# Causal attention on one core: PSUM banks given out by a model of their readers, and maxima, exponentials and masks taken two or four heads at a time

## The chip, the cores and the metric

The kernel runs on one core of a Trainium2 chip. The metric is the device time of one launch in microseconds (us). The engines that matter are TensorE (PE, which multiplies matrices into the eight banks of PSUM; PEld is its loading of weights), VectorE (DVE) and ScalarE (ACT), which read PSUM, GpSimd (POOL), which here works on SBUF, and SyncE (SP), which issues DMAs. Each engine has its own instruction stream; an instruction that waits holds up all that stand behind it in that stream.

## The reference

One layer of a transformer on x of 2048 tokens by 256 features, in float32:

```python
q = x @ Wq;  c_kv = x @ Wkv_down;  k = c_kv @ Wk_up;  v = c_kv @ Wv_up    # 16 heads of 16
q, k: the last 12 of the 16 numbers of a head are rotated by their position
scores = (q . k) / 4, with -inf where the key is after the query
out = softmax(scores) . v
x = layernorm(x + out)
x = layernorm(x + experts(x) + shared(x))     # 16 experts, each token to its best two
```

## The kernel before, in words

**Tiling.** The 2048 tokens are four chunks (`c`) of 512. The 16 heads are four groups (`g`) of four heads. A head has 16 numbers and is padded to 32 partitions, so that the four heads of a group fill the 128 partitions. A product of one head uses 32 of TensorE's 128 rows, so that the products of the four heads of a group can run side by side in four row groups. Float32 products are done in passes; the trace has two records for one product.

**Two kinds of work.** Softmax needs the largest score of each query before the exponentials. `Maxima(g, c, t, kc)` is for one block `t` of 128 queries and one chunk `kc` of keys: four products of queries by keys (one for each head, tile `m`, 128 queries on partitions by `n` keys), and the maximum of each on DVE into `pm` (line L490). On the diagonal (`kc == c`) only `n = 128 (t + 1)` keys count, and one DVE operation adds a mask to all `n` columns and takes the maximum (L485; a short read of the accumulator follows each). `shift` turns the maxima and adds them to the queries (tile `qa`, L508), so that the later product has them already subtracted. `Weighted(g, c, kb, ...)` is for one block `kb` of 128 keys and one chunk of 512 queries: four products (tile `s`, 128 keys by 512 queries, fewer on the diagonal, where they begin at column `n0`), the exponential of each on ACT into an SBUF tile `p` of the pool `wkp` (L535), and on the diagonal a select on POOL which clears the upper triangle of a 128x128 block of `p` (L539).

**Values one step late.** `values` multiplies the four `p` by the values: four products into one bank (tile `av`). ACT copies `av` to `avs` the first time (L559), later to `more` (L566), which POOL adds to `avs` (L567); in steps with no Maxima DVE adds straight from PSUM (L563).

**The order.** The attention is a list, written out by hand, of 180 `steps`: each has a Maxima, a Weighted, or both. TensorE's instructions are kept in program order (`pe`, L139 to L143; every product has line L140 in the profile). A step with both goes

```python
for some, others in (((0, 1), (2, 3)), ((2, 3), (0, 1))):
    s.products(some)
    m.products(others)
    s.exponentials()
    m.reductions()
```

and then come `prior.values(...)`, the values of the step before, and what the table `at` puts behind this step: the loading and projection of later chunks and groups (`prologue`, `project_k`, `project_q`, `project_v`), `shift`, `finish`, and the routing of the experts.

**The banks.** `bank()` (L397) takes a tile of one bank, [128, 512] float32, from a pool of eight (`ps_sc`, L293), round robin. A step with both kinds takes eight for its products, and `av` takes a ninth. The pool `wkp` (L292) has nine tiles of 512 columns.

The experts follow after the attention, from about 593 us on; the change does not touch them.

Of the kernel before, what the change touches and what calls it, by code (L numbers as in the profile page):

```python
# [10 lines left out]
F32 = mybir.dt.float32  # L11
I32 = mybir.dt.int32
AF = mybir.ActivationFunctionType
ALU = mybir.AluOpType
AX = mybir.AxisListType
PSUM = bass.MemoryType.PSUM

P = 128
S, E = 2048, 256
H, HD, LAT = 16, 16, 64  # L20
NOPE, RD = 4, 12
G = 4
PAD = 32
LOW = HD + NOPE
# [17 lines left out]
SCALE = 0.25  # L42
EPS = 1e-5
NEG = -1.0e30


@with_exitstack
def block_kernel(
# [237 lines left out]
    with ExitStack() as att:  # L286
# [2 lines left out]
        wk1 = att.enter_context(tc.tile_pool(name="wk1", bufs=1))  # L289
        wk2 = att.enter_context(tc.tile_pool(name="wk2", bufs=2))  # L290
        wk3 = att.enter_context(tc.tile_pool(name="wk3", bufs=3))
        wkp = att.enter_context(tc.tile_pool(name="wkp", bufs=9))  # L292
        ps_sc = att.enter_context(tc.tile_pool(name="ps_sc", bufs=8, space=PSUM))  # L293

        wqs = [ap1.tile([P, 2, P], F32, tag=f"wqs{g}", name=f"wqs{g}") for g in range(G)]

# [97 lines left out]

        qs, ks, vs, qa, pm, avs = {}, {}, {}, {}, {}, {}

        def bank(name):  # L397
            return ps_sc.tile([P, CH], F32, tag="sc", name=name)

        def prologue(c):  # L400

            copy = nc.scalar.copy if c else nc.vector.tensor_copy
            for k in range(2):
                pt = bank(f"pt{c}_{k}")
                for t in range(4):
                    transpose(pt[:, t * P : (t + 1) * P], xr[c][:, t, k * P : (k + 1) * P], ident)
                copy(xT[c][:, k, :], pt)
            pc = bank(f"pc{c}")
            for k in range(2):
                matmul(  # L410
                    pc, lhsT=wkds[:, k, :], rhs=xT[c][:, k, :], start=(k == 0), stop=(k == 1)
                )
            copy(ckv[c], pc)
# [25 lines left out]

        def project_v(g, c):  # L440

            pv = [bank(f"pv{g}_{c}_{a}") for a in range(2)]
            for b in range(4):
                a = b % 2
                r = slice(a * LAT, (a + 1) * LAT)
                matmul(
                    pv[a][:, (b // 2) * P : (b // 2 + 1) * P],
                    lhsT=ckv[c][r, b * P : (b + 1) * P],
                    rhs=wvs[r, g * P : (g + 1) * P], start=True, stop=True,
                )  # L450
            v = kv.tile([P, CH], F32, tag="v", bufs=6, name=f"v{g}_{c}")
            for a in range(2):
                nc.scalar.copy(
                    v.rearrange("p (b a m) -> p b a m", a=2, m=P)[:, :, a, :],
                    pv[a][:, : 2 * P].rearrange("p (b m) -> p b m", m=P),
                )
            nc.gpsimd.memset(v.rearrange("p (h d) -> p h d", d=PAD)[:, :, ONE : ONE + 1], 1.0)
            vs[g, c] = v

        class Maxima:  # L460


            def __init__(self, g, c, t, kc):
                self.g, self.c, self.t, self.kc = g, c, t, kc
                self.n = CH if kc < c else (t + 1) * P
                if (g, c) not in pm:
                    pm[g, c] = wk3.tile([P, 4, 4, NCH], F32, tag="pm", name=f"pm{g}_{c}")

            def products(self, heads):
                g, c, t, kc, n = self.g, self.c, self.t, self.kc, self.n  # L470
                self.ps = {}
                for j in heads:
                    r = PAD * j
                    self.ps[j] = bank(f"m{g}_{c}_{t}_{kc}_{j}")
                    matmul(
                        self.ps[j][:, :n], lhsT=qs[g, c][r : r + PAD, t * P : (t + 1) * P],
                        rhs=ks[g, kc][r : r + PAD, :n], start=True, stop=True,
                    )

            def reductions(self):  # L480
                t, kc, n = self.t, self.kc, self.n
                for j, ps in self.ps.items():
                    to = pm[self.g, self.c][:, t, j, kc : kc + 1]
                    if kc == self.c:
                        nc.vector.tensor_tensor_reduce(  # L485
                            out=ps[:, :n], in0=ps[:, :n], in1=qmask[:, CH - n :], scale=1.0,
                            scalar=3.0 * NEG, op0=ALU.add, op1=ALU.max, accum_out=to,
                        )
                    else:
                        nc.vector.tensor_reduce(to, ps, AX.X, ALU.max)  # L490

        def negated(g, c):
            nm = wk1.tile([P, 4, 4, PAD], F32, tag="nm", name=f"nm{g}_{c}")
# [16 lines left out]
        class Weighted:  # L510
# [3 lines left out]
            def __init__(self, g, c, kb, first, last):  # L514
                self.g, self.c, self.kb, self.first, self.last = g, c, kb, first, last
                self.n0 = max(0, kb - 4 * c) * P
                self.pr = {}

            def products(self, heads):
                g, c, kb, n0 = self.g, self.c, self.kb, self.n0  # L520
                self.ps = {}
                for j in heads:
                    r = PAD * j
                    self.ps[j] = bank(f"s{g}_{c}_{kb}_{j}")
                    matmul(
                        self.ps[j][:, n0:],
                        lhsT=ks[g, kb // 4][r : r + PAD, (kb % 4) * P : (kb % 4 + 1) * P],
                        rhs=qa[g, c][r : r + PAD, n0:], start=True, stop=True,
                    )

            def exponentials(self):
                g, c, kb, n0 = self.g, self.c, self.kb, self.n0
                for j, ps in self.ps.items():
                    pr = wkp.tile([P, CH], F32, tag="pr", name=f"p{g}_{c}_{kb}_{j}")
                    nc.scalar.activation(pr[:, n0:], ps[:, n0:], AF.Exp, scale=SCALE)  # L535
                    if kb >= 4 * c:

                        diag = pr[:, n0 : n0 + P]
                        nc.gpsimd.affine_select(  # L539
                            out=diag, in_=diag, pattern=[[1, P]], base=0, channel_multiplier=-1,  # L540
                            compare_op=ALU.is_ge, fill=0.0,
                        )
                    self.pr[j] = pr

            def values(self, alone):


                g, c, kb, n0 = self.g, self.c, self.kb, self.n0
                pv = bank(f"av{g}_{c}_{kb}")
                for j in range(4):  # L550
                    r = PAD * j
                    o = (kb % 4) * P + r
                    matmul(
                        pv[r : r + PAD, n0:], lhsT=vs[g, kb // 4][:, o : o + PAD],
                        rhs=self.pr[j][:, n0:], start=True, stop=True,
                    )
                if self.first:
                    avs[g, c] = wk2.tile([P, CH], F32, tag="avs", name=f"avs{g}_{c}")
                    nc.scalar.copy(avs[g, c], pv)  # L559
                    return  # L560
                to = avs[g, c][:, n0:]
                if alone:
                    nc.vector.tensor_tensor(to, to, pv[:, n0:], ALU.add)  # L563
                else:
                    more = wk2.tile([P, CH], F32, tag="more", name=f"more{g}_{c}_{kb}")
                    nc.scalar.copy(more[:, n0:], pv[:, n0:])  # L566
                    nc.gpsimd.tensor_tensor(to, to, more[:, n0:], ALU.add)  # L567

        def finish(g, c):
            po = ps_sc.tile([P, 4, 4, PAD], F32, tag="sc", name=f"po{g}_{c}")  # L570
            for t in range(4):
                transpose(
                    po[:, t].rearrange("p h d -> p (h d)"), avs[g, c][:, t * P : (t + 1) * P], ident
                )
            rs = wk2.tile([P, 4, 4, 1], F32, tag="rs", name=f"rs{g}_{c}")
            nc.vector.reciprocal(rs, po[:, :, :, ONE : ONE + 1])
            oh = wk2.tile([P, 4, 4, HD], F32, tag="oh", name=f"oh{g}_{c}")
            nc.vector.tensor_tensor(oh, po[:, :, :, :HD], rs.to_broadcast([P, 4, 4, HD]), ALU.mult)
            xg = xr[c][:, :, g * 4 * HD : (g + 1) * 4 * HD]
            adder = nc.vector if g == G - 1 else nc.gpsimd  # L580
            adder.tensor_tensor(xg, xg, oh.rearrange("p t h d -> p t (h d)"), ALU.add)
            if g == G - 1:
                for t in range(4):
                    st = wk2.tile([P, 6], F32, tag="st", name=f"st{c}_{t}")
                    nc.vector.bn_stats(st, xr[c][:, t, :E])
                    nc.vector.bn_aggr(mv[:, 4 * c + t, :], st)
# [129 lines left out]
        while step < len(steps) or prior or at:  # L716
            m, s = steps[step] if step < len(steps) else (None, None)
            m = m and Maxima(*m)
            s = s and Weighted(*s, step == s_first[s[:2]], step == s_last[s[:2]])
            if m and s:  # L720
                for some, others in (((0, 1), (2, 3)), ((2, 3), (0, 1))):

                    s.products(some)
# [371 lines left out]
```

## Time and profile before

| | |
|---|---|
| time, median of 3 runs | 808.76 us (806.41 to 810.42) |
| profiled execution: time | 803.1 us |
| profiled execution: span, mean granted TensorE clock | 801.1 us, 0.993 |
| instructions | 14999 |
| exponentials (L535), ACT | 640, 292.6 us busy, 540 ns mean |
| maxima off the diagonal (L490), DVE | 384, 237.5 us, 681 ns |
| masked maxima (L485), DVE | 256, 118.3 us, 521 ns |
| selects (L539), POOL | 256, 70.5 us, 297 ns |

All durations come from the one profiled execution. Its span is the time from the first to the last instruction; the time of the same execution is 2.0 us longer, and the median of the runs is 5.7 us above that time. "Busy" is the sum over an engine's instructions; neighbours on one engine can overlap in the records, since one instruction begins before the result of the one ahead of it is wholly written. A row of the form `out<-in` names the tiles that an instruction writes and reads; an arrow `<-` after an idle time names what the engine waited for.

### The profile page before, as it was taken

Reading aid. Unit: us, or ns where it says so; the run is one execution under the profiler, and the core shown is the slowest. Engines: PE = TensorE matmul, PEld = TensorE weight load, DVE = VectorE, ACT = ScalarE, POOL = GpSimd, SP = SyncE. Lnnn points to the kernel's source line nnn. Section 1 sums busy time; section 2 is a strip of 40 time slices with the busy share of each in tenths; the row PEclk is TensorE's granted clock in tenths of the full one; section 3 lists DMA queues with packets and bytes.
Section 4 is the critical chain, followed back from the end, with each engine's and each line's share of the span. In section 5 each row is a group of like instructions: output and inputs, shape, how many; then the busy total and the mean of one; then the engine's idle time right before and its main releaser. Section 6 shows DMA issues by size and latency. Waiting matters only on the chain. (4 is left out here: it accounts for less than half of the span.)

```text
span 801.1 us, 14999 instructions
## 1 busy us (share of the span) xinstructions
PE 771.5 (96%) x5086; PEld 361.3 (45%) x5086; DVE 547.1 (68%) x1489; ACT 445.0 (56%) x997; POOL 323.0 (40%) x557
## 2 busy tenths in 40 slices
PE   7999999999999999999999999999989899999985
PEld 3443433444333344543334453444336466666543
DVE  2768888887687887777788678788775433333276
ACT  1143646377775786766688668875742033333345
POOL 2032524434355454635455454461661333333300
PEclk9999999999999999999999999999999999999998
DMA  5469999991000000001000000000225322222172
GB/s 147 130 174 327 310 301 304 294 301 54 2 1 1 1 2 1 2 19 37 1 2 2 1 2 2 1 2 2 80 84 141 107 80 86 82 86 70 37 230 85
DMA packets 67378, 71.88 MB, mean 90 GB/s; under 512 B 4736, under 2 KB 61539, under 8 KB 67302
## 3 DMA queue, kind: packets, MB, share of 16 engines
q1 hardware_dynamic: 62286, 61.77, 27.7%
q0 software_dynamic: 3552, 8.43, 3.0%
q10 hardware_dynamic: 1464, 0.72, 0.4%
q8 instruction: 41, 0.67, 0.4%
q14 instruction: 35, 0.29, 0.1%
HBM read 26.44 MB, written 45.78 MB: 90 GB/s over the span
## 5 line engine op out<-in xcount | busy, mean ns | idle before, releaser
L535 ACT ACTIVATE p<-s 128x512 f32<-128x512 f32 (+3 forms) x640 | 292.6, 540 | 128.2 <-PE m L140 79.0
L140 PE MATMUL m<-k,q 32*128 32x512 f32 (+3 forms) x1280 | 303.9, 566 | 0.8 <-DVE rot L423 0.5
L140 PE MATMUL s<-qa,k 32*128 32x512 f32 (+3 forms) x1280 | 279.4, 556 | 1.8 <-DVE avs L563 0.7
L490 DVE TENSOR_REDUCE pm<-m 128x1 f32<-128x512 f32 x384 | 237.5, 681 | 44.4 <-PE m L140 44.0
L567 POOL TENSOR_TENSOR avs<-avs,more 128x512 f32<-128x512 f32 (+3 forms) x125 | 136.7, 1094 | 167.3 <-ACT more L566 163.8
L140 PEld LDWEIGHTS s<-qa,k 32*128 32x128 f32 x1280 | 107.1, 184 | 117.6 <-ACT p L535 67.6
L140 PE MATMUL av<-p,v 128*32 128x512 f32 (+3 forms) x1280 | 154.2, 540 | 1.9 <-DVE base L244 1.2
L140 PEld LDWEIGHTS m<-k,q 32*128 32x128 f32 x1280 | 122.7, 184 | 44.5 <-issue 11.9
L485 DVE CUSTOM_DVE_ANT_0 m<-m,qmask 128x512 f32<-128x512 f32 (+3 forms) x256 | 118.3, 521 | 29.1 <-PE m L140 26.1
L566 ACT COPY more<-av 128x512 f32<-128x512 f32 (+3 forms) x125 | 65.6, 525 | 38.3 <-PE av L140 30.4
L539 POOL TENSOR_SCALAR_AFFINE_SELECT p<-p 128x128 f32<-128x128 f32 x256 | 70.5, 297 | 38.2 <-ACT p L535 36.4
L931 POOL DMA_INDIRECT yg<-yb,to x42 | 41.4, 985 | 88.2 <-ACT yb L923 44.1
L140 PEld LDWEIGHTS av<-p,v 128*32 128x32 f32 x1280 | 27.1, 108 | 104.1 <-ACT p L535 54.2
L140 PE MATMUL ph<-w,xbT 128*128 x168 | 60.3, 482 | 2.4 <-DVE xbT L884 1.7
L903 DVE TENSOR_TENSOR rh<-ru,ph 128x176 f32<-128x176 f32 x42 | 14.2, 338 | 53.7 <-ACT ru L901 53.7
L140 PE MATMUL h<-xT,cs 128*128 128x512 f32 (+1 forms) x96 | 43.6, 599 | 4.9 <-DVE sh L794 2.0
L901 ACT ACTIVATE ru<-ph 128x176 f32<-128x176 f32 x42 | 13.3, 318 | 59.3 <-PE ph L140 59.3
L140 PE MATMUL py<-w2r,hT 88*128 x168 | 43.4, 380 | 0.7 <-ACT hT L910 0.7
L278 POOL DMA_INDIRECT xg<-xr,slot x32 | 31.1, 971 | 31.1 <-issue 19.8
L140 PEld LDWEIGHTS ph<-w,xbT 128*128 128x128 f32 x168 | 28.5, 189 | 20.8 <-issue 11.6
L428 POOL TENSOR_TENSOR k<-rot 128x512 f32<-128x512 f32 x16 | 20.3, 1267 | 42.5 <-DVE rot L426 42.5
L140 PEld LDWEIGHTS py<-w2r,hT 88*128 88x128 f32 x168 | 31.7, 189 | 12.0 <-ACT hT L910 1.2
(147 smaller groups left out, 633.3 us busy)
## 6 DMA issues: line engine op xcount, KB each, us to landing
xg<-hot SPq DMA_DIRECT2D x16, 2064.0 KB
w<-in_w_dram SPq DMA_DIRECT2D x4, 1408.0 KB
xb<-xg SPq DMA_DIRECT2D x42, 129.0 KB
got<-yg SPq DMA_DIRECT2D x8, 512.0 KB
w2r<-in_w_dram SPq DMA_DIRECT2D x2, 1408.0 KB
xr<-in_x_dram SPq DMA_DIRECT2D x4, 512.0 KB
out_dram<-o SPq DMA_DIRECT2D x8, 256.0 KB
cs<-in_rope_dram SPq DMA_DIRECT2D x16, 80.0 KB
```

Source lines behind the costliest of these rows:

```text
L140: tc.keep_in_program_order(op(*args, **kw))
L278: put = nc.gpsimd.indirect_dma_start(out=xg[:, :], out_offset=bass.IndirectOffsetOnAxis(ap=slot[:, j, i : i + 1], axis=0), in_=xr[c][:, t, ...
L428: nc.gpsimd.tensor_tensor(ks[g, c], tmp[:, 0, :], tmp[:, 1, :], ALU.add)
L485: nc.vector.tensor_tensor_reduce(out=ps[:, :n], in0=ps[:, :n], in1=qmask[:, CH - n :], scale=1.0, scalar=3.0 * NEG, op0=ALU.add, op1=ALU.m ...
L490: nc.vector.tensor_reduce(to, ps, AX.X, ALU.max)
L535: nc.scalar.activation(pr[:, n0:], ps[:, n0:], AF.Exp, scale=SCALE)
L539: nc.gpsimd.affine_select(out=diag, in_=diag, pattern=[[1, P]], base=0, channel_multiplier=-1, compare_op=ALU.is_ge, fill=0.0,)
L566: nc.scalar.copy(more[:, n0:], pv[:, n0:])
L567: nc.gpsimd.tensor_tensor(to, to, more[:, n0:], ALU.add)
L901: nc.scalar.activation(u, ph[:, :INTER], AF.Silu)
L903: nc.vector.tensor_tensor(us[b], u, ph[:, INTER:], ALU.mult)
L931: nc.gpsimd.indirect_dma_start(out=yg[:, :], out_offset=bass.IndirectOffsetOnAxis(ap=to[:, 0:1], axis=0), in_=yb, in_offset=None, bounds_c ...
```

## The change

- One PSUM tile of eight banks is taken once. A class `Banks` decides, while the program is being built, which banks each product gets: it keeps a model of TensorE, DVE and ACT (a product costs its columns times 7/8, a read its columns times 3/4 on ACT or 1 on DVE plus `LEAD`), and gives the banks that come free first by it; for two heads it looks for two neighbours, for four heads for four neighbours or two pairs.
- The exponentials of two heads become one instruction over two neighbouring banks, into a tile of [128, 2, 512]; where two banks are not neighbours, there are two. The select takes two heads. `wkp` has five double tiles.
- The maxima of two heads become one reduction, where their banks are neighbours (`runs` finds neighbours among the banks taken).
- On the diagonal the mask is first added in place, to the last 128 columns of up to four heads in one DVE instruction, and then the plain maxima are taken.
- A step with both kinds whose Maxima is on the diagonal has another order: all four Maxima products, their masks and maxima, then all four Weighted products and their exponentials. The other steps keep their order.

```diff
+BANKS, PAIRS = 8, 5
+def runs(taken, longest=BANKS):
...
+class Banks:
+    LEAD = 96
+    def product(self, columns):
+        self.at["pe"] += columns * 7 // 8
+    def take(self, n):
+        now = self.at["pe"]
+        def ready(b):
+            return max(self.free[b], now)
+        single = sorted(range(BANKS), key=ready)[:n]
+        taken = sorted(single)
...
+            when, side = min(ways)
+            if when <= max(map(ready, single)) + 2 * self.LEAD:
+                taken = side
...
+    def read(self, banks, reader, columns):
+        cost = columns * (3 if reader == "act" else 4) // 4 + self.LEAD
+        self.at[reader] = max(self.at[reader], self.at["pe"] + self.LEAD) + cost
+        for b in banks:
+            self.free[b] = self.at[reader]
...
-        wkp = att.enter_context(tc.tile_pool(name="wkp", bufs=9))
-        ps_sc = att.enter_context(tc.tile_pool(name="ps_sc", bufs=8, space=PSUM))
+        wkp = att.enter_context(tc.tile_pool(name="wkp", bufs=PAIRS))
+        ps_sc = att.enter_context(tc.tile_pool(name="ps_sc", bufs=1, space=PSUM))
+        banks = Banks(ps_sc.tile([P, BANKS, CH], F32, tag="sc", name="banks"))
...
             def reductions(self):
...
-                        nc.vector.tensor_tensor_reduce(
-                            out=ps[:, :n], in0=ps[:, :n], in1=qmask[:, CH - n :], scale=1.0,
-                            scalar=3.0 * NEG, op0=ALU.add, op1=ALU.max, accum_out=to,
-                        )
-                    else:
-                        nc.vector.tensor_reduce(to, ps, AX.X, ALU.max)
+                    for _, taken in self.ps:
+                        for b, k in runs(taken):
+                            of = banks.tile[:, b : b + k, n - P : n]
+                            nc.vector.tensor_tensor(
+                                of, of, qmask[:, CH - P :].unsqueeze(1).to_broadcast([P, k, P]),
+                                ALU.add,
+                            )
+                            banks.read([], "dve", k * P)
+                for j, taken in self.ps:
+                    for b, k in runs(taken, 2):
+                        nc.vector.tensor_reduce(
+                            to[:, t, j : j + k, kc], banks.tile[:, b : b + k, :n], AX.X, ALU.max
+                        )
+                        banks.read(range(b, b + k), "dve", k * n)
+                        j += k
...
             def exponentials(self):
...
-                    pr = wkp.tile([P, CH], F32, tag="pr", name=f"p{g}_{c}_{kb}_{j}")
-                    nc.scalar.activation(pr[:, n0:], ps[:, n0:], AF.Exp, scale=SCALE)
...
+                    for h in range(0, len(taken), 2):
+                        pr = wkp.tile([P, 2, CH], F32, tag="pr", name=f"p{g}_{c}_{kb}_{j}")
+                        i = 0
+                        for b, k in runs(taken[h : h + 2]):
+                            nc.scalar.activation(
+                                pr[:, i : i + k, n0:], banks.tile[:, b : b + k, n0:], AF.Exp,
+                                scale=SCALE,
+                            )
...
             def values(self, alone):
...
-                pv = bank(f"av{g}_{c}_{kb}")
+                (b,) = banks.take(1)
+                pv = banks.tile[:, b, :]
...
-            if m and s:
+            if m and s and m.kc == m.c:
+
+                m.products(range(4))
+                m.reductions()
+                s.products(range(4))
+                s.exponentials()
+            elif m and s:
```

## The prediction

> **What bounds the kernel now.** I read the page's busy shares first, then the clock by slices, the engines' busy time by stretches, and the timeline of one step.
>
> ```profile
> PE 771.5 (96%) x5086; PEld 361.3 (45%) x5086; DVE 547.1 (68%) x1489; ACT 445.0 (56%) x997; POOL 323.0 (40%) x557
> PEclk9999999999999999999999999999999999999998
> 160.00:535.00 375.00, 373.34 (x3024) 156.66 (x3022) 295.68 (x736) 272.33 (x600) 183.41 (x320) 1.00 0.08 23
> ```
>
> TensorE is busy 96% of the span. The third line is the middle of the attention: of 375 us, TensorE is busy 373.3, DVE 295.7, ACT 272.3, POOL 183.4, at granted clock 1.00. The readers have slack there. The next view is the timeline of a whole step (both kinds, off the diagonal, each product 512 columns); columns are start, length, engine, line, operation.
>
> ```profile
> 401.75 0.70 PE L140 MATMUL s<-qa,k 32*128 32x512 f32 x2
> 402.91 2.07 ACT L535 ACTIVATE p<-s 128x512 f32<-128x512 f32 x4 [0.38 <-PE m L140]
> 402.99 2.48 DVE L490 TENSOR_REDUCE pm<-m 128x1 f32<-128x512 f32 x4 [0.44 <-PE m L140]
> 403.15 0.59 PE L140 MATMUL s<-qa,k 32*128 32x512 f32 x2
> 403.68 0.16 PEld L140 LDWEIGHTS av<-p,v 128*32 128x32 f32 x8 [0.76 <-ACT p L535]
> 403.68 1.06 PE L140 MATMUL av<-p,v 128*32 128x512 f32 x8
> 404.68 0.66 PE L140 MATMUL pn<-ident,nm 128*128 128x128 f32 x4
> ```
>
> The eight products start at 401.75, `av` at 403.68 (the block: 1.93), and the next work at 404.68: 2.93 a step with no gap. The first exponential starts 1.16 after the step and the four take 2.07; the reductions take 2.48. ACT then sat idle 0.38 and DVE 0.44. What matters is the ninth bank: `av` takes the bank of this step's first `s`, which its single exponential leaves at +1.16 + 0.60 = +1.76, before `av` is due at +1.93. In the trace, a matmul follows the end of such a read by 0.06.
>
> A diagonal step 512 wide, from the timeline:
>
> ```profile
> 405.26 0.70 PE L140 MATMUL s<-qa,k 32*128 32x512 f32 x2
> 406.48 2.07 ACT L535 ACTIVATE p<-s 128x512 f32<-128x512 f32 x4 [1.03 <-PE m L140]
> 407.19 1.06 PE L140 MATMUL av<-p,v 128*32 128x512 f32 x8
> 408.19 0.70 PE L140 MATMUL s<-qa,k 32*128 32x512 f32 x2
> ```
>
> Same shape: first exponential at +1.22, `av` at +1.93. The last rows are groups kept apart by shape (count | busy us, mean ns | idle):
>
> ```profile
> L535 ACT ACTIVATE p<-s 128x512 f32<-128x512 f32 x448 | 233.1, 602 | 109.6 <-PE m L140 71.5 <-PE s L140 37.0
> L535 ACT ACTIVATE p<-s 128x384 f32<-128x384 f32 x64 | 27.0, 500 | 5.0 <-PE s L140 2.5 <-PE m L140 1.9
> L535 ACT ACTIVATE p<-s 128x256 f32<-128x256 f32 x64 | 19.5, 391 | 8.7 <-PE m L140 4.0 <-PE s L140 2.8 <-issue 1.9
> L535 ACT ACTIVATE p<-s 128x128 f32<-128x128 f32 x64 | 13.2, 293 | 4.9 <-PE s L140 3.2 <-PE m L140 1.6
> L490 DVE TENSOR_REDUCE pm<-m 128x1 f32<-128x512 f32 x384 | 237.5, 681 | 44.4 <-PE m L140 44.0
> L508 DVE TENSOR_TENSOR qa<-q,pn 128x512 f32<-128x512 f32 x16 | 10.8, 677 | 3.3 <-PE pn L140 3.3
> L563 DVE TENSOR_TENSOR avs<-avs,av 128x128 f32<-128x128 f32 x3 | 0.8, 281 | 0.7 <-PE av L140 0.7
> PEld av L140 <- ACT p L535: 54.2, 81, 0.8
> ```
>
> The last line is the chain of waits of the weight loads: `av`'s loads already look to an exponential more than to anything else.
>
> **Prices of the wider reads.** ACT: (602 - 293) / 384 = 0.805 ns a column, so 2x512 columns last 0.602 + 512 x 0.805 = 1.01 us, 2x384 0.81, 2x256 0.60, 2x128 0.39. A pair saves what one instruction costs beyond its columns: four take 2.07, so one follows another by (2.07 - 0.60) / 3 = 0.489, of which 0.412 is columns: 0.077. DVE: (683 - 281) / 384 = 1.05 ns a column (the 512 form of L563 is 683), so a pair of 512 lasts 1.22; four take 2.48, pitch 0.60, saving 0.064 a pair. The mask on four heads, 512 columns in all, is nearest to L508: 0.68.
>
> What is saved lies in slack: the instruction list of the changed kernel has 294 exponentials of two banks in place of 588 single ones (26 pairs stay split), and 286 paired reductions. 294 x 0.077 = 23 us of ACT and 286 x 0.064 = 18 us of DVE, beside a TensorE that is busy 373 of 375 us. Selects by two (297 ns each now, 0.3 to 0.6 by two) are cleared on POOL before the values one step later; nothing.
>
> The Trainium skill ("Perfetto Trace Analysis", section "Optimizing Scalar/DVE Operations") gives an access overhead of about 125 ns for DVE and 51 ns for Scalar on PSUM; by it the savings would be 36 us and 15 us, as far off the path as mine. The same section speaks against this change: engines that are not saturated but cause bubbles elsewhere may do better with instructions broken up, because work is then done sooner. The rows above (idle 0.38 and 0.44 a step) put this kernel in that case.
>
> **A, whole steps (75).** The list of waits in the changed program says who frees `av`'s bank: in 74 of 75 this step's first pair of exponentials. It starts at +1.16 as before (its two products are still the first wave), ends at +2.17, and `av` follows at +2.23 instead of +1.93: 0.30 a step, at most 22 us. Some steps of the trace are already late for other reasons: 57 of the 75 have a block under 2.23, and what they lack to it is 14.1 us together. **+14** (9 to 22).
>
> **B, diagonal steps (59).** All Maxima products now go first, so the `s` products end the block and the first exponential starts at its end + 0.08 instead of in its middle. `av` waits for that pair in 46 of them and for the first paired maximum in 13 (mask from +1.16, 0.68, then 1.22: +3.06, the same within 0.1). With nothing free, `av` is late by 0.08 + pair + 0.06: 1.15, 0.95, 0.74 and 0.53 us for widths 512, 384, 256, 128. The shortest blocks of the trace are 1.93, 1.67, 1.45 and 1.20; what steps already have above these is taken off, which leaves means of 1.07, 0.69, 0.67 and 0.38. There are 14 steps of each width: 15.0 + 9.6 + 9.4 + 5.4 = 39.4; three more, with `s` 512 wide, add 2.3. **+42** (25 to 50; lower if part of it would have been waited out anyway a step later).
>
> **C, work behind `av`.** In 13 places the projection or chain placed after `av` must reuse a bank of the same step, mostly `av`'s own, behind its copy (0.59 by L566, and 0.1 of passing on): 13 x 0.7 = **+9** (3 to 15).
>
> **D, what gets shorter.** 16 steps have only Maxima and are paced by DVE: two pairs save 0.13 each, 2 us. Banks chosen by who is free in place of round robin may spare some of the stalls of the first 160 us, where loads and short chains cost some 30 us over an unbroken TensorE: 2 more. **-4** (-15 to 0).
>
> **E, second effects.** The next step's products want the banks of the second reduction, which by my times ends at +3.6 against a next wave at +3.7. It is close: **+2** (0 to 15). The five double tiles of `wkp` hold ten heads against nine before; no wait.
>
> Sum: 14 + 42 + 9 - 4 + 2 = +63. The profiled execution of 803.1 would become 866; the median lies 5.7 above it: **871 us**.
>
> A second page of the skill ("TensorE: Matmul & The Clock Gate", on psum-queue depth-cycling) warns that small idle gaps between groups of matmuls can make the clock oscillate. The clock row shows full speed in every slice but the last, the first 160 us with their broken stream among them, so I price it at nothing; if the new stalls did halve the clock over a tenth of the attention, that would be 57 us more.
>
> **Rivals.**
> - *The readers set the pace, and fewer instructions win (faster).* If TensorE's full stream were stretched by its readers, ACT's 23 us or the waits for exponentials (54 us in the row above, though most are loads waiting in advance beside running matmuls) would count. About -19: **790**. It decides if the first pair leaves its bank by +1.87, that is, if it lasts 0.71 or less; two singles in a row take 1.09 today. 8%.
> - *The stall is partly absorbed.* Diagonal steps cost no more than whole ones (0.30), because the model's free banks or a shorter read help: 14 + 59 x 0.3 + 2 - 4 = +30: **839**. 14%.
> - *Row groups fall out of step.* With four banks freed at different times, the four heads' products begin one by one and a wave of 0.43 us is lost in two thirds of the 134 combined steps: +38 on my sum: **910**. 8%.
> - *Little happens*, stalls and savings cancel: 2%. That the pairs aren't there is excluded by the 294 of 320.
>
> **How the numbers follow.** My forecast has 68%. Its own bounds, not all at one end, are +27 to +93. The range, 830 to 902, takes these in and the absorbed case, and leaves out the rivals at both ends and the tails. The three runs of before span 4 us, so 0.5% (4 us) is what can be told from no change. Faster 8%, same 2%, slower 90%.
>
> **What would show it.** In the profile after, exponentials of 2x512 should last 1.01 us and reductions 1.22; whole steps 3.23 instead of 2.93, with `av` 0.06 behind the first pair; diagonal steps 512 wide about 4.1, `av` at +3.1; TensorE's busy share down to about 89%, clock unchanged; the experts, from their start on, 208 us as before. I am wrong if `av` starts before the first pair's end (no bank shared), if a pair of 512 lasts under 0.8 us, or if the attention's end stays at 593 us.

## The result, and the profile after

The change makes the kernel slower: 900.78 us, median of 4 runs (896.59 to 901.54), against 808.99 us. The ratio is 1.1128 (95% interval 1.1084 to 1.1172). The forecast was 871 us with a range of 830 to 902: the sign held, and so did the mechanism named for the steps with both kinds; the size is at the range's upper end, and 43 of the 98.7 us below come from places where the forecast had 7 in all. The profiled execution took 901.54 us with a span of 899.8, against 801.1 before: 98.7 us more.

The page's busy shares, its clock row, and the stretch from 160 to 535 us, as before (the attention now lasts until 692 us, so the stretch holds less work: 2524 records of products in place of 3024):

```profile
PE 777.6 (86%) x5086; PEld 343.6 (38%) x5086; DVE 567.2 (63%) x1031; ACT 434.1 (48%) x703; POOL 305.5 (34%) x429
PEclk8999999999999999999999999997789999999999
160.00:535.00 375.00, 320.66 (x2524) 123.82 (x2524) 262.76 (x337) 218.92 (x322) 143.28 (x190) 1.00 0.09 24
```

ACT has 294 instructions fewer and DVE 458, as the change promises, and it buys nothing: TensorE, which was busy 373 of these 375 us, is now busy 321. Over the whole execution ACT is busy 11 us less (434.1 against 445.0), but DVE 20 us more (567.2 against 547.1): the maxima and their masks, now instructions of their own, take 377.1 us (329.6 in L569, 47.5 in L562), where they took 359.6 with the masked maxima fused (237.5 in L490, 122.1 in L485). The clock row shows two things to come back to, an 8 in the first slice and 7, 7, 8 near the end of the attention.

The timeline of the whole step shown before (now at 459.30), one row for each stage:

```profile
459.30 0.70 PE L205 MATMUL banks<-qa,k 32*128 32x512 f32 x2
460.48 1.94 ACT L625 ACTIVATE p<-banks 128x1024 f32<-128x1024 f32 x2 [0.40 <-PE banks L205]
460.56 2.36 DVE L569 TENSOR_REDUCE pm<-banks 128x2 f32<-128x1024 f32 x2 [0.76 <-PE banks L205]
461.55 1.07 PE L205 MATMUL banks<-p,v 128*32 128x512 f32 x8 [0.25 <-ACT p L625]
462.56 0.65 PE L205 MATMUL banks<-ident,nm 128*128 128x128 f32 x4
```

The first pair starts at +1.18 and lasts 1.02 (group row below), so it ends at +2.20; `av` (out `banks`, in `p,v`) follows at +2.25 in place of +1.93, and its row names ACT's `p` as what it waited for. In 68 of the 75 whole steps the block now lies between 2.20 and 2.45 us; before, 46 were under 2.10.

The diagonal step shown before, now at 463.32:

```profile
463.32 1.14 PE L205 MATMUL banks<-k,q 32*128 32x512 f32 x8
464.29 1.04 PE L205 MATMUL banks<-qa,k 32*128 32x512 f32 x8
464.53 0.70 DVE L562 TENSOR_TENSOR banks<-banks,qmask 128x512 f32<-128x512 f32 x1 [0.53 <-PE banks L205]
465.27 2.36 DVE L569 TENSOR_REDUCE pm<-banks 128x2 f32<-128x1024 f32 x2
465.44 1.94 ACT L625 ACTIVATE p<-banks 128x1024 f32<-128x1024 f32 x2 [2.17 <-PE banks L205]
466.55 1.07 PE L205 MATMUL banks<-p,v 128*32 128x512 f32 x8 [1.23 <-DVE pm L569]
```

All Maxima products go first, then the `s` products; the mask takes 0.70, the first paired maximum ends near +3.2, and `av` starts at +3.23 where it started at +1.93. TensorE stands still for 1.23 us. Here DVE's pair was the releaser; ACT's first pair (465.44 and 1.02 long) ends at about the same time.

The prices of the wider reads were right, from the groups by shape (count | busy, mean ns):

```profile
L625 ACT ACTIVATE p<-banks 128x1024 f32<-128x1024 f32 x214 | 211.0, 1022 | 148.6 <-PE banks L205 137.7 <-DVE pm L569 6.8 <-POOL avs L667 1.6
L569 DVE TENSOR_REDUCE pm<-banks 128x2 f32<-128x1024 f32 x191 | 227.1, 1222 | 77.7 <-PE banks L205 76.7
L562 DVE TENSOR_TENSOR banks<-banks,qmask 128x512 f32<-128x512 f32 x44 | 30.8, 699 | 32.4 <-PE banks L205 27.9 <-ACT v L524 4.0
```

Following the trace step by step (a block is from a step's first product to `av`; "behind the block" is `av` and what the table `at` puts after it), the span divides so:

| part | before | after | difference | forecast |
|---|---|---|---|---|
| ahead of the first step | 19.9 | 23.0 | +3.1 | 0 |
| blocks of whole steps | 160.1 | 177.7 | +17.6 | +14 |
| blocks of diagonal steps | 103.9 | 142.0 | +38.1 | +42 |
| behind the block, both kinds | 175.3 | 197.3 | +22.0 | +11 (C 9, E 2) |
| steps with both kinds but no `av` | 23.4 | 22.1 | -1.3 | -2 |
| steps of Maxima alone | 52.7 | 57.0 | +4.3 | -2 |
| steps of Weighted alone (the end of the attention) | 57.2 | 72.7 | +15.5 | 0 |
| experts and rest | 208.7 | 208.0 | -0.7 | 0 |

### The profile page after: what moved, and what is told of

Same layout as the page of the kernel before. It is cut to its first block, busy times and chain, and to the rows that moved or that the text cites. A ratio compares the mean times of both kernels' runs of the same rounds, so it can differ in the third digit from the quotient of the medians.

```text
span 899.8 us, 14108 instructions
## 1 busy us (share of the span) xinstructions
PE 777.6 (86%) x5086; PEld 343.6 (38%) x5086; DVE 567.2 (63%) x1031; ACT 434.1 (48%) x703; POOL 305.5 (34%) x429
## 5 line engine op out<-in xcount | busy, mean ns | idle before, releaser
L569 DVE TENSOR_REDUCE pm<-banks 128x2 f32<-128x1024 f32 (+4 forms) x354 | 329.6, 973 | 79.5 <-PE banks L205 76.7
L625 ACT ACTIVATE p<-banks 128x1024 f32<-128x1024 f32 (+5 forms) x346 | 274.6, 840 | 215.6 <-PE banks L205 199.5
L205 PE MATMUL banks<-qa,k 32*128 32x512 f32 (+3 forms) x1280 | 248.4, 575 | 15.8 <-DVE rot L494 3.9
L205 PE MATMUL banks<-k,q 32*128 32x512 f32 (+3 forms) x1280 | 236.1, 566 | 12.8 <-DVE pm L569 5.3
L205 PE MATMUL banks<-p,v 128*32 128x512 f32 (+3 forms) x1280 | 156.6, 560 | 62.3 <-ACT p L625 44.4
L205 PEld LDWEIGHTS banks<-qa,k 32*128 32x128 f32 x1280 | 97.7, 190 | 119.2 <-issue 35.5
L205 PEld LDWEIGHTS banks<-k,q 32*128 32x128 f32 x1280 | 81.7, 183 | 75.0 <-DVE pm L569 26.8
L666 ACT COPY more<-banks 128x512 f32<-128x512 f32 (+3 forms) x125 | 64.6, 517 | 43.8 <-PE banks L205 33.8
L634 POOL TENSOR_SCALAR_AFFINE_SELECT p<-p 128x256 f32<-128x256 f32 x128 | 51.4, 407 | 94.8 <-ACT p L625 93.2
L562 DVE TENSOR_TENSOR banks<-banks,qmask 128x512 f32<-128x512 f32 (+2 forms) x84 | 47.5, 569 | 42.4 <-PE banks L205 36.9
L205 PEld LDWEIGHTS ph<-w,xbT 128*128 128x128 f32 x168 | 28.5, 189 | 20.4 <-issue 11.3
```

The lines of the kernel that those rows point to most:

```text
L205: tc.keep_in_program_order(op(*args, **kw))
L562: nc.vector.tensor_tensor(of, of, qmask[:, CH - P :].unsqueeze(1).to_broadcast([P, k, P]), ALU.add,)
L569: nc.vector.tensor_reduce(to[:, t, j : j + k, kc], banks.tile[:, b : b + k, :n], AX.X, ALU.max)
L625: nc.scalar.activation(pr[:, i : i + k, n0:], banks.tile[:, b : b + k, n0:], AF.Exp, scale=SCALE,)
L634: nc.gpsimd.affine_select(out=diag, in_=diag, pattern=[[0, 2], [1, P]], base=0, channel_multiplier=-1, compare_op=ALU.is_ge, fill=0.0,)
```

## The experiments

Two theories were set up on this table. Theory 1: `av` waits for wide reads of this step's banks (the two block rows, +56). Theory 2: the model gives out banks that are still being read while older ones lie free (the other rows, +43). The rivals stand in the expectations. Each run has its own runs of the kernel before on the same chip (medians 807.25, 806.69 and 811.46 us for the three groups); ratios are to these.

**The old order of diagonal steps.**

```diff
-            if m and s and m.kc == m.c:
-                m.products(range(4))
-                m.reductions()
-                s.products(range(4))
-                s.exponentials()
-            elif m and s:
+            if m and s:
```

> The change with one part undone: steps with a diagonal Maxima get back the order of the other steps (two s, two m, two s, two m). Theory 1, late release: av waits for the first pair of exponentials, and in the new order that pair starts only behind the whole block. Then the diagonal blocks fall from 3.00, 2.58, 2.11 and 1.78 us (512 to 128 wide) to about 2.25, 1.95, 1.6 and 1.3, some 35 us together: 865 us. Rival, the bank that av gets or the mask and paired maximum on DVE set the end in any order: within 8 us of the change, 893 to 905.

868.42 us, ratio 1.0755 (1.0713 to 1.0796). The diagonal blocks fell from 142.0 to 111.2 us and whole blocks stayed at 179.9. Theory 1 holds for the diagonal: with the `s` products in front again, the first pair starts in the middle of the block, and about a third of the loss is gone. The same edit on two other versions below gives about as much or more: 1.0854 to 1.0491 with ties broken by age, and 951.44 to 891.57 us with banks given out by age alone.

**Ties of the model broken by age.**

```diff
-            return max(self.free[b], now)
+            return max(self.free[b], now), self.age[b]
...
+        self.turn += 1
...
+            self.age[b] = self.turn
```

> The change with another rule where the model holds several banks for free: the one taken longest ago, in place of the lowest number (or the one beside the bank that comes free last). Theory 2, bank choice: the model's clocks leave out DMA waits, the routing chain on DVE and half the length of the projections, so that banks it holds for free are still being read, and TensorE waits for a bank just used while older ones lie free; this makes the 43 us that steps with no pairing at issue and the work behind av have gained (start 3, Maxima alone 4, Weighted alone 15, work behind av 22). By it the time falls by 20 to 35 us, to 866 to 881. Rival, all of the loss is late release: 895 to 905.

875.15 us, ratio 1.0854 (1.0811 to 1.0896). The work behind the blocks fell from 197.3 to 176.8 us (175.3 before the change), the steps of Weighted alone from 72.7 to 65.6, the start from 23.0 to 19.9; the blocks stayed. Theory 2 holds as far as ties go. What such a pick looks like in the change (TensorE's rows of its timeline):

```profile
209.47 0.48 PE L205 MATMUL banks<-wvs,ckv 64*128 64x128 f32 x2
210.40 0.71 PE L205 MATMUL banks<-wvs,ckv 64*128 64x128 f32 x6 [0.44 <-DVE q L509]
211.36 0.70 PE L205 MATMUL banks<-qa,k 32*128 32x512 f32 x2 [0.26 <-ACT v L524]
```

The rest of `project_v` was given the bank that `project_q` had just filled, and waits for DVE to read it; then the next step's products are given the bank of `v` itself. Before, with round robin, these followed without a gap.

**The bank model alone.** No paired reads are left, and the order is the old one.

```diff
-                        for b, k in runs(taken[h : h + 2]):
+                        for b, k in runs(taken[h : h + 2], 1):
...
+                    if kc == self.c:
+                        nc.vector.tensor_tensor_reduce(
+                            out=banks.tile[:, b, :n], in0=banks.tile[:, b, :n],
+                            in1=qmask[:, CH - n :], scale=1.0, scalar=3.0 * NEG,
+                            op0=ALU.add, op1=ALU.max, accum_out=to[:, t, j, kc : kc + 1],
+                        )
+                    else:
+                        nc.vector.tensor_reduce(
+                            to[:, t, j, kc : kc + 1], banks.tile[:, b, :n], AX.X, ALU.max
+                        )
...
```

> The bank model alone: exponentials and maxima one head at a time, masked maxima fused as before, the old order everywhere; banks given out by the model. Theory 2 (the model gives banks that are still read): slower than before by 15 to 40 us, 825 to 850, with the steps of Weighted alone at 70 us in place of 57. Rival (the model is as good as round robin or better, the pairs do all the harm): 800 to 812.

840.88 us, ratio 1.0422 (1.0380 to 1.0465): 34 us slower than round robin with not one wide read, as theory 2 has it. The steps of Weighted alone took 61.7 us, not the 70 expected; the rest lies in whole steps (280.2 in all, against 267.4) and diagonal ones (209.2 against 195.3).

**The first pair split.**

```diff
-            def exponentials(self):
+            def exponentials(self, first=2):
...
-                        for b, k in runs(taken[h : h + 2]):
+                        for b, k in runs(taken[h : h + 2], first if j == 0 else 2):
...
-                s.exponentials()
+                s.exponentials(first=1)
```

> The change with the first two heads of the exponentials of each step with both kinds taken one by one again; everything else, the paired tiles too, stays. Theory 1: av finds a bank 0.4 us earlier; whole blocks fall from 2.25 to about 1.95 (75 x 0.28 = 21 us), diagonal ones by up to 0.4 where the exponentials and not DVE freed the bank (46 x 0.3 = 14): 866 us, although ACT has 134 instructions more. Rival, ACT's or DVE's count of instructions matters: more ACT instructions, 905 or more.

899.22 us, ratio 1.1142 (1.1101 to 1.1184). The expectation failed. Diagonal blocks did fall, by 15 us (142.0 to 126.7), but whole blocks rose by 6 (177.7 to 184.1) and split into two kinds: 27 under 2.10 us, as theory 1 has it, and 30 of 2.75 or more. The work behind the blocks rose by 8 as well (197.3 to 205.7). The model sees other read times and picks other banks; what a block of 2.75 or more is, the last four runs below show. It isn't the count of instructions: ACT has 125 more than in the change, and the time is the same.

**Age alone, and with it the old order, and the split.** The model's clocks are gone; a pair is the two neighbours taken longest ago (four banks are two such pairs).

```diff
-        now = self.at["pe"]
...
+        single = sorted(range(BANKS), key=self.age)[:n]
         if n == 1:
...
+            taken = single
+        elif n == 2:
+            taken = min(([b, b + 1] for b in range(BANKS - 1)), key=lambda w: max(map(self.age, w)))
...
```

> The change with the model's clocks gone: neighbours are given out by age alone, the pair or the bank taken longest ago. Everything else stays as in the change. Theory 2 (what the model lacks is age; its clocks earn nothing beyond that): within 10 us of the model with ties broken by age, 865 to 885. Rival, its clocks do find banks that are free earlier, and age alone gives pairs that are still read: 890 or more.

> Two parts undone together: the old order of diagonal steps, and banks by age alone. Theories 1 and 2 are separate causes and add up: 900.8 - 32 - 26 = 843 (836 to 850). Rival, they are one and the same wait, mended by either: 865 to 870.

> As the run before, and the first two heads' exponentials one by one as well. Theory 1: av finds the bank of a single exponential at +1.76 again, whole blocks go from about 2.25 to 1.95 (75 x 0.3) and diagonal ones by less: 20 to 30 us under the run before, 812 to 824, near the kernel before though half of the exponentials, all reductions and all masks are still taken together. Rival, taking two at once does its harm elsewhere (neighbours that must both be free): 835 to 850.

951.44 us (ratio 1.1813, 1.1773 to 1.1852), 891.57 (1.1055, 1.1019 to 1.1092) and 860.02 (1.0681, 1.0643 to 1.0718). The first expectation failed and its rival held: where pairs are given out, the model's clocks do earn something. The second can't be read as a test of adding up, since age alone costs 50 us by itself. A whole step of age alone shows how:

```profile
489.54 0.70 PE L191 MATMUL banks<-qa,k 32*128 32x512 f32 x2
490.72 1.98 ACT L611 ACTIVATE p<-banks 128x1024 f32<-128x1024 f32 x2
491.79 1.13 PE L191 MATMUL banks<-k,q 32*128 32x512 f32 x4 [0.25 <-ACT p L611]
492.85 1.06 PE L191 MATMUL banks<-p,v 128*32 128x512 f32 x8
```

Not `av` but the last two Maxima products got the banks of the first pair. They were due beside the last `s` products, at +0.98; they start at +2.25, when the first paired exponential (from 490.72, 1.02 long) has left these banks, and run 1.06 us by themselves: `av` at +3.31. Forty-one of the whole steps have a block of 2.75 us or more. But in the third run everything is as in the second except the split, and it is 31.5 us less: of the 24 whole blocks of 2.20 to 2.45 two are left (21 are under 2.10); of the 45 blocks of 3.30 and more, 34 now lie between 2.86 and 3.01, because the late Maxima product waits for one exponential where it waited for two, and 12 stay above 3.3. By age the banks do not depend on the readers, so this is the late release measured with the order held; about 7.5 us of it are waits of `av` in the 24, 14.5 us waits of Maxima products in the 45, and 9.5 us are in the diagonal blocks. In the three runs the steps of Weighted alone take 58.0, 57.0 and 58.0 us: with age they are what they were before (57.2), with all exponentials paired in the first two. So that row is not the pairs' by themselves; the model alone makes it 61.7, the model giving out pairs 72.7.

**Values between the halves, in the kernel before.**

```diff
                     m.reductions()
+                    if prior:
+                        prior.values(alone=False)
+                        prior = None
```

> The kernel before with one edit: in steps with both kinds the values of the step before come between the two halves of the products instead of behind them. The ninth bank is then taken by a Maxima product about 1 us later, and the copy of av is over earlier. If the kernel before still loses time on that ninth bank (whole blocks 2.00 on average against 1.93 at best): 3 to 8 us faster, 800 to 805. If not, or if the products' row groups or the exponentials of the step before come too late: the same or slower, 806 to 825.

854.65 us, ratio 1.0603 (1.0577 to 1.0629), from 6 runs.

```profile
428.69 2.06 ACT L535 ACTIVATE p<-s 128x512 f32<-128x512 f32 x4 [0.41 <-PE m L140]
429.46 1.41 PE L140 MATMUL av<-p,v 128*32 128x512 f32 x8
429.82 0.14 PEld L140 LDWEIGHTS av<-p,v 128*32 128x32 f32 x2 [0.22 <-ACT p L535]
430.80 0.70 PE L140 MATMUL s<-qa,k 32*128 32x512 f32 x2
```

The values of heads 2 and 3 now come 1 us earlier than their exponentials can be done: the last weights wait for `p`, and 1.00 us of `av` becomes 1.34. Over 134 combined steps that would be 46 us, and by the trace these steps together take 47 us more (486.2 against 439.3). Moving the ninth bank from `av` to a Maxima product is no way out.

**Old order and ties by age, then the split, then no paired exponentials, then no paired reads at all.** All four keep the model with ties by age and have the old order of diagonal steps; each adds to the one ahead of it.

> The change with the old order of diagonal steps, and the model kept but its ties broken by age. It replaces the test of whether theories 1 and 2 add up that was spoiled by giving banks by age alone (which cost 50 us by itself). Adding up: 900.8 - 32.4 - 25.6 = 843 (836 to 850). Rival, one wait that either edit mends: 865 or more.

> As the run before, with the first two heads' exponentials one by one. By age alone the same edit was worth 31.5 us (891.6 to 860.0). Theory 1: 20 to 30 us under the run before, 813 to 823. Rival, the edit helps only where banks are given badly: within 8 us of the run before.

> Old order, ties by age, all exponentials one by one: of the pairing only the paired maxima and the four-head masks are left. If DVE's part is harmless (it has slack, and the banks it frees are wanted a step later): 805 to 815. If a pair of maxima keeps banks too long: 820 or more.

> The bank model alone, with ties broken by age: exponentials and masked maxima one by one, old order. It is the version that could beat the kernel before, if choosing banks by their readers is worth anything once the ties go to the oldest: theory 2 says 33 us of the model's harm are its ties and clocks, so 803 to 815; below 800 only if round robin's own waits (whole blocks 2.00 against 1.93, work behind av) are mended as well. Rival, the clocks themselves are wrong, and ties don't matter here: 835 to 842 as without the edit.

| kernel | us | ratio (95%) | whole blocks, sum | of 75: under 2.10, 2.20 to 2.45, 2.75 and more |
|---|---|---|---|---|
| old order, ties by age | 850.59 | 1.0491 (1.0459 to 1.0523) | 180.7 | 0, 58, 4 |
| and first pair split | 851.86 | 1.0489 (1.0457 to 1.0520) | 183.2 | 26, 6, 30 |
| and all exponentials single | 851.00 | 1.0496 (1.0463 to 1.0530) | 189.3 | 22, 4, 41 |
| and all maxima single, masks fused | 845.68 | 1.0423 (1.0398 to 1.0448) | 184.6 | 27, 3, 32 |
| kernel before | | 1 | 160.1 | 46, 3, 3 |

The first expectation held on the ratio: the two edits add up, 1.1128 - 0.0373 - 0.0274 = 1.048. The other three failed. The rival held for the split (within 8 us of the run before), for all exponentials single by its number (over 820), though not by its reason, since single maxima then give back only 5 us, and for the model alone by its ratio: 1.0423 with ties by age, 1.0422 without, so that with single reads the tie rule is worth nothing. All three failed in one way: taking reads apart moves whole steps from the middle column to the first and the last, and the sum hardly changes. A step of the last column, in the last kernel:

```profile
417.66 2.07 ACT L624 ACTIVATE p<-banks 128x512 f32<-128x512 f32 x4 [0.38 <-PE banks L207]
417.91 0.59 PE L207 MATMUL banks<-qa,k 32*128 32x512 f32 x2
418.31 1.12 PE L207 MATMUL banks<-k,q 32*128 32x512 f32 x2
419.36 1.06 PE L207 MATMUL banks<-p,v 128*32 128x512 f32 x8
```

One Maxima product of the last wave was given the bank of the first exponential, which comes free 0.60 after 417.66. In the kernel before, the products of this wave begin together at +0.98, here 417.48; this one starts at 418.31, 0.83 us late and by itself, and takes 1.05 us: 2.86 for a block of 1.93. `av`, which is due at +1.93 and could have had this bank without waiting, got the one that the Maxima product should have had. Round robin deals them the right way round. The code says why the model does not. Its TensorE does one product after the other: by it the last two Maxima products begin after the last `s` products, at 1344 columns or about +1.45 us (four products of 512 are 896 columns, and 0.97 us in the trace). And for two heads `take` accepts neighbours up to 2 x `LEAD` = 192 columns, 0.2 us, later than the best two banks. By the model that bank is free at 1472 columns, inside this tolerance. Followed through the kernel's own code, the model gives a Maxima product of the last wave the first exponential's bank in 32 whole steps, and these are the same 32 that have a block of 2.75 us or more; in the step shown, two other banks were free by the model, but not neighbours. Neither the order of products in the model nor the tolerance was varied by itself, so why it picks so is read from code and trace. What the picks cost is shown: of the 40 us by which the profiled execution is longer (span 841.4 against 801.1), 24.5 are longer blocks of whole steps.

No version tried beats the kernel before. Paired reads with banks given out round robin were not tried; age alone is the nearest to it.

## Why the prediction was right, and where it was too small

**Terms that held.** A (whole steps, +14 forecast, +17.6 measured) and B (diagonal steps, +42 and +38.1): `av` sits 0.05 behind the first pair at +2.25 (+2.23 forecast), and the pairs last 1.02 and 1.22 as worked out. The old order alone gave back 32 us, and the split, with the order of banks held, 31.5, most of it from waits of Maxima products that the forecast did not have. The rival that fewer instructions help was not seen anywhere: 125 more ACT instructions in the split made no difference to the time. The forecast also had DVE save 18 us; it is busy 20 us more, because the sum priced the pairs and left out that mask and maximum, one instruction before, are now two; but that lies in slack.

**The step that failed** is the belief that the model's choice could at worst do no harm outside of those blocks. Term D put it at -4 with bounds of -15 and 0, so with no loss at all. The gain hoped for in the first 160 us is there in the steps with no `av` (-1.3), but the start and the steps of Maxima alone, which lie there too, lost 7.4: 3.1 ahead of the first step, and 4.3 where 2 were to be gained (D counted 16 such steps, those off the diagonal; there are 20). Terms C and E put 11 us behind `av`, C with 13 places, and the row is 22: C counted the banks that must be shared, not those shared by choice. The steps of Weighted alone stood at nothing and cost 15.5. In all, the rows outside the blocks had +7 and measured +43. That the time still lies inside the range is in part luck: the forecast's own sum ended at +93 for the profiled execution, which became 98.4 longer (803.1 to 901.5), and what filled the room above +63 was not what its bounds stood for. Ties by age took back 26 us, nearly all of it in these rows, and age alone all of the 15.5. By ratios, the runs give a path from the kernel before to the change: the model with ties by age and single reads +0.042, all pairs +0.007, ties by number +0.026, the new diagonal order +0.037. The parts depend on the path: with ties by number from the start, the model is +0.042 as well, and all pairs +0.033 (1.0422 to 1.0755).

**Two causes that hide each other.** The pairs' +0.007 is not the price of pairing. In whole steps a paired read makes `av` wait 0.3 us; with single reads the same model puts a Maxima product into the same bank and loses 0.93 us in fewer steps. Either way 20 to 29 us go to longer whole blocks (the sums of the table above, less 160.1), and of the kernels tried only round robin with single reads avoids both. My rival of row groups falling out of step (910 us, 8%) described the second mechanism, at half its price, and put it in the wrong kernel: in the change 3 whole blocks last 2.75 us or more, as before.

**The clock.** I priced the clock at nothing on the strength of a full row. The row was misread: a 9 stands for 90% or more, and in the kernel before the clock stood at half twice in the first 160 us (the last three columns of these rows are the granted clock, the busy share of the DMA engines, and GB/s):

```profile
28.50:31.80 3.30, 3.30 (x10) 2.04 (x9) 1.91 (x11) 1.17 (x2) 0.00 (x0) 0.50 0.30 90
107.00:110.30 3.30, 3.30 (x17) 1.68 (x20) 2.11 (x5) 0.00 (x0) 1.06 (x2) 0.50 1.10 309
535.00:593.00 58.00, 55.77 (x429) 23.40 (x422) 42.69 (x175) 37.97 (x86) 26.59 (x54) 1.00 0.11 38
```

It was not nothing. In the change the granted clock over the last 73 us of the attention (619 to 692) was 0.81, against 1.00 in the same work before (the row above), and 0.85 over the first 23 us against 1.00:

```profile
602.00:615.40 13.40, 9.59 (x86) 4.08 (x84) 11.55 (x25) 6.92 (x13) 6.00 (x10) 1.00 0.00 1
615.50:619.00 3.50, 2.58 (x24) 1.29 (x22) 3.17 (x12) 0.77 (x2) 1.20 (x3) 0.50 0.01 2
619.00:692.00 73.00, 64.22 (x424) 24.09 (x420) 43.32 (x166) 35.85 (x46) 23.65 (x37) 0.81 0.08 30
```

At the start it can be seen at work; the first row is `project_q` in the kernel before, the others are the change:

```profile
13.31 1.98 PE L140 MATMUL pq<-xT,wqs 128*128 128x512 f32 x4
12.23 1.13 PE L205 MATMUL banks<-ckv,wks 64*128 64x512 f32 x4 [0.83 <-issue]
14.53 0.75 DVE L494 SCALAR_TENSOR_TENSOR rot<-banks,unit,cs 128x512 f32<-128x512 f32 x1 [2.40 <-DMA cs<-in_rope_dram]
15.38 3.75 PE L205 MATMUL banks<-xT,wqs 128*128 128x512 f32 x4 [2.02 <-issue]
```

`project_q` is given the bank that L494 still has to read, and L494 waits for a late DMA. TensorE stands still for 2.02 us, until that read ends at 15.28 (the profile names no releaser; that it is this bank follows from the kernel's code, which here gives out two banks in turn while the other six have not been used), and then the four products take 3.75 where they took 1.98 before. The granted clock is 1.00 from 13.4 to 14.7 us, inside the wait, and 0.50 from 14.8 to 15.3. At the end of the attention it is 1.00 from 602.0 to 615.4 and 0.50 from 615.5 to 619.0, with no wait of TensorE above 1.01 us between 602.0 and 615.5; later waits there reach 2.0 us.

Over four of the kernels the steps of Weighted alone go with the clock there: 57.0 us at 0.97, 58.0 at 0.94, 65.6 at 0.86, 72.7 at 0.81; but the model alone takes 61.7 at 0.97. So part of their 15.5 us is waiting and part is products at a lower clock; 73 x 0.19 = 14 us is the most that the clock can have had of it, and the runs don't separate the two. The Trainium skill ("TensorE: Matmul & The Clock Gate", section "HAM oscillation — how this bites in real kernels") warns of idle gaps above about 3.4 us. Here the clock fell within a gap of 2.02 us and after waits of at most 1.01 us, and in the kernel before it fell at 28 us with no wait above 0.25 us in the 8 us ahead of it. So in this case the clock fell without such a gap, and the measurement decides.

## What to carry to other kernels

On an engine that was off the path, wider reads saved nothing here, and what they held was released later: look for who wants the first half of it, and when. The Trainium skill's sentence on breaking up instructions ("Perfetto Trace Analysis", section "Optimizing Scalar/DVE Operations") agrees with the 31.5 us that splitting one pair gave back, but only once the banks' order was held still. When buffers are given out by a model, test the giver alone against round robin, with nothing else changed: here that was a third of the loss, and it also changed what the other experiments meant.

## What was not expected of the hardware

TensorE's clock was lowered around waits of 2 us and less: the four products of `project_q` took 3.75 us in place of 1.98 at the start, and the granted clock was 0.81 on average over the 73 us at the end of the attention, where it first fell after waits of at most 1.01 us. In the kernel before it stood at 0.50 from 28.5 to 31.8 us and from 107.0 to 110.3 although TensorE had hardly waited. And one product that has missed its wave takes 1.05 us by itself (418.31 to 419.36), as long as four together in the kernel before (0.95 us, from +0.98 to +1.93).
